# Four-layer vision network: layers 3 and 0 of neighbouring images run as one row of chunks, two scan states per instruction

## Chip, cores and metric

The kernel runs on one core of a Trainium2 chip. The metric is the device time of one execution in microseconds (us); smaller is better. Engine names follow the profile: PE is TensorE (matmuls; PEld are its weight loads), DVE is VectorE, ACT is ScalarE, POOL is GpSimd, SP is the queue that issues DMAs.

## What is computed

Four images of 64 channels and 64 x 64 pixels go through four layers, all in float32:

```python
x = layer0(x)   # cross-shaped conv, relu, layernorm, mamba with 16 states, + residual
x = layer1(x)   # two mambas with 96 states, along rows and along columns, + residual
x = layer2(x)   # content-dependent 3x3 high-pass filter, + residual
x = layer3(x)   # mamba with 16 states, projection, layernorm, silu, + residual

# the mamba of layers 0 and 3, per image (L = 4096 tokens, d_inner = 128, 16 states):
xz = h @ in_proj.T; xm, z = split(xz)
xc = silu(causal_conv4(xm) + b)
dt, B, C = split(xc @ x_proj.T)            # 4, 16 and 16 columns
dt = softplus(dt @ dt_proj.T + b)
for t in range(L):                         # A = -exp(A_log)
    h = h * exp(dt[t] * A) + (dt[t] * xc[t]) * B[t]
    y[t] = h @ C[t]
y = (y + xc * D) * silu(z)
```

The state of layer 0 begins at zero for each image. That of layer 3 runs on from image to image, because its reference flattens the batch into one sequence; so do the three tokens that its convolution looks back to.

## The kernel before

Images are done one after the other: `image(b)` calls `layer0`, `layer1`, `layer2`, `layer3`. Layers 0 and 3 hold the tokens of an image in 8 chunks of 512 (`TOK`), channels on partitions. They share two functions.

`mamba_front` makes, for one chunk, what the scan needs: the convolution (4 matmuls into `pc`), the gate (`pz`), both silus in one tile of 128 x 1024 (`sl`), the step size (`pd`, then a softplus as a polynomial of degree 6 on DVE) and `wx`, the product of step size and input.

`mamba_scan` goes through the 16 states of the chunk one by one. For each state PE makes two broadcasts over the partitions, B into `pb` and C into `pq`, each a 128 x 128 by 128 x 512 matmul with a weight tile `xb` whose columns are all the same. ACT makes the decay `a` (an exponential), DVE makes `g` = `pb` times `wx`, the scan `h` along the tokens, and `o` = `pq` times `h`. POOL saves the last column of `h` as the state and adds `o` to `y`. Broadcast tiles rotate over four PSUM banks, `a`, `g`, `h` and `o` over three buffers each.

`layer0` wraps this with the cross-shaped convolution (5 matmuls, `px`), relu (`seq`), the layernorm (`pm`, `pv`, `rsqrt_eps`) in front, and behind it the output projection `po`, the residual into `x1`, and a transposed copy on POOL. `layer3` adds the projection `po`, a layernorm, a silu, the residual on POOL and the DMA to the output behind each chunk. In both, the front of chunk c + 1 is traced before the scan of chunk c, and the tile framework's scheduler orders the instructions of an engine from there. Layer 1 alone fixes its order: `in_order` ties each instruction of PE, DVE, ACT and POOL to the one traced before it on that engine.

A matmul in float32 leaves two records in the trace, one for each of two passes over its columns.

Of the kernel before, what the change touches and what calls it, by code (L numbers as in the profile page):

```python
# [20 lines left out]
HW = H * W  # L21
# [33 lines left out]
LOG1P = (  # L55
    0.9999987483024597,
    -0.4998696446418762,
    0.3310944736003876,
    -0.23503851890563965,
    0.1492237150669098,  # L60
    -0.0664016604423523,
    0.014140978455543518,
)


class Net:
    def __init__(self, ctx, tc, a):
        self.tc, self.nc, self.a = tc, tc.nc, a
        nc = self.nc
        self.const = ctx.enter_context(tc.tile_pool(name="const", bufs=1))  # L70
        self.xp = ctx.enter_context(tc.tile_pool(name="xp", bufs=1))
        with tc.tile_pool(name="setup", bufs=1) as sp, tc.tile_pool(
            name="setup_ps", bufs=2, space=PSUM
        ) as pp:
            self.setup(sp, pp)
        for b in range(NB):
            self.image(b)
# [25 lines left out]

    def silu(self, out, v, t):

        nc = self.nc
        nc.scalar.activation(t, v, AF.Abs)
        nc.scalar.activation(t, t, AF.Exp, scale=-1.0)
        nc.scalar.activation(t, t, AF.Ln, bias=1.0)
        nc.vector.scalar_tensor_tensor(t, v, 0.0, t, ALU.min, ALU.subtract)  # L110
        nc.scalar.activation(t, t, AF.Exp)
        nc.vector.tensor_tensor(out, v, t, ALU.mult)  # L112

    def softplus_steps(self, out, v, u, p):

        nc = self.nc

        def first():
            nc.scalar.activation(u, v, AF.Abs)
            nc.scalar.activation(u, u, AF.Exp, scale=-1.0)  # L120

        def second():
            nc.vector.tensor_scalar(p, u, LOG1P[6], LOG1P[5], ALU.mult, ALU.add)
            nc.vector.tensor_tensor(p, p, u, ALU.mult)
            for c in LOG1P[4:1:-1]:
                nc.vector.scalar_tensor_tensor(p, p, c, u, ALU.add, ALU.mult)

        def third():
            for c in LOG1P[1::-1]:
                nc.vector.scalar_tensor_tensor(p, p, c, u, ALU.add, ALU.mult)  # L130
            nc.vector.scalar_tensor_tensor(out, v, 0.0, p, ALU.max, ALU.add)

        return [first, second, third]
# [98 lines left out]
    def setup_mamba(self, sp, pp, n):  # L232
# [23 lines left out]
        m["xbc"] = self.load(self.const, f"{n}_xbc", [DIN, 2 * NST])  # L256
# [115 lines left out]
    def image(self, b):  # L372
        self.use_exp()
        x1 = self.layer0(b)
        x2 = self.layer1(b, x1)
        self.use_exp()
        x3 = self.layer2(b, x2)
        self.layer3(b, x3)


    def mamba_pools(self, ctx, n):
        tc = self.tc
        p = {}
        p["w"] = ctx.enter_context(tc.tile_pool(name=f"{n}_w", bufs=1))
        p["s"] = ctx.enter_context(tc.tile_pool(name=f"{n}_s", bufs=2))
        p["n"] = ctx.enter_context(tc.tile_pool(name=f"{n}_n", bufs=3))
        p["bc"] = ctx.enter_context(tc.tile_pool(name=f"{n}_bc", bufs=4, space=PSUM))
        p["ps"] = ctx.enter_context(tc.tile_pool(name=f"{n}_ps", bufs=4, space=PSUM))
        return p

    def mamba_bcast(self, p, m, n):

        t = p["w"].tile([DIN, 2 * NST, DIN], F32, name=f"{n}_xb", tag="xb")
        self.nc.vector.tensor_copy(t, m["xbc"].unsqueeze(2).to_broadcast([DIN, 2 * NST, DIN]))
        return t

    def mamba_front(self, p, m, src, n):

        nc = self.nc
        vec = m["vec"]  # L400
        pc = p["ps"].tile([DIN, TOK], F32, name=f"{n}_pc", tag="ps")
        for k in range(4):
            self.mm(pc, m["wk"][:, k, :], src(k), k == 0, k == 3)
        v = p["s"].tile([DIN, 2, TOK], F32, name=f"{n}_v", tag="v")
        nc.scalar.activation(v[:, 0, :], pc, AF.Identity, bias=vec[:, 4:5])
        pz = p["ps"].tile([DIN, TOK], F32, name=f"{n}_pz", tag="ps")
        self.mm(pz, m["wz"], src(3))
        nc.scalar.copy(v[:, 1, :], pz)
        t = p["s"].tile([DIN, 2, TOK], F32, name=f"{n}_t", tag="t")
        s = p["s"].tile([DIN, 2, TOK], F32, name=f"{n}_sl", tag="sl")  # L410
        self.silu(s, v, t)
        xc, sz = s[:, 0, :], s[:, 1, :]
        pd = p["ps"].tile([DIN, TOK], F32, name=f"{n}_pd", tag="ps")
        self.mm(pd, m["wdt"], xc)
        dv = p["s"].tile([DIN, TOK], F32, name=f"{n}_dv", tag="dv")
        nc.vector.tensor_scalar(dv, pd, vec[:, 5:6], None, ALU.add)
        u = p["s"].tile([DIN, TOK], F32, name=f"{n}_u", tag="u")
        q = p["s"].tile([DIN, TOK], F32, name=f"{n}_q", tag="q")
        dl = p["s"].tile([DIN, TOK], F32, name=f"{n}_dl", tag="dl")
        for step in self.softplus_steps(dl, dv, u, q):  # L420
            step()
        wx = p["s"].tile([DIN, TOK], F32, name=f"{n}_wx", tag="wx")
        nc.vector.tensor_tensor(wx, dl, xc, ALU.mult)
        return xc, dl, wx, sz

    def mamba_scan(self, p, m, xb, f, n):

        nc = self.nc
        xc, dl, wx, sz = f
        y = p["s"].tile([DIN, TOK], F32, name=f"{n}_y", tag="y")  # L430
        nc.gpsimd.tensor_scalar(y, xc, m["vec"][:, 6:7], None, ALU.mult)
        for i in range(NST):
            pb = p["bc"].tile([DIN, TOK], F32, name=f"{n}_pb{i}", tag="bc")
            self.mm(pb, xb[:, i, :], xc)
            pq = p["bc"].tile([DIN, TOK], F32, name=f"{n}_pq{i}", tag="bc")
            self.mm(pq, xb[:, NST + i, :], xc)
            a = p["n"].tile([DIN, TOK], F32, name=f"{n}_a{i}", tag="a")
            nc.scalar.activation(a, dl, AF.Exp, scale=m["A"][:, i : i + 1])  # L438
            g = p["n"].tile([DIN, TOK], F32, name=f"{n}_g{i}", tag="g")
            nc.vector.tensor_tensor(g, pb, wx, ALU.mult)  # L440
            h = p["n"].tile([DIN, TOK], F32, name=f"{n}_h{i}", tag="h")
            st = m["state"][:, i : i + 1]
            nc.vector.tensor_tensor_scan(h, a, g, st, ALU.mult, ALU.add)  # L443
            nc.gpsimd.tensor_copy(st, h[:, TOK - 1 : TOK])
            o = p["n"].tile([DIN, TOK], F32, name=f"{n}_o{i}", tag="o")
            nc.vector.tensor_tensor(o, pq, h, ALU.mult)  # L446
            nc.gpsimd.tensor_tensor(y, y, o, ALU.add)  # L447
        yz = p["s"].tile([DIN, TOK], F32, name=f"{n}_yz", tag="yz")
        nc.vector.tensor_tensor(yz, y, sz, ALU.mult)
        return yz  # L450

    def layer0(self, b):
# [3 lines left out]
        for r in range(0, H, 16):  # L456
            nc.sync.dma_start(xin[:, 1 + r : 17 + r, 1 : W + 1], self.a["x"][b, :, r : r + 16, :])

        x1 = self.xp.tile([2 * C, H + 3, W + 3], F32, name=f"x1_{b}", tag="xb")
        nc.gpsimd.memset(x1, 0.0)  # L460
        nc.vector.memset(self.m0["state"], 0.0)
        with ExitStack() as ctx:
            p = self.mamba_pools(ctx, f"a{b}")
            xb = self.mamba_bcast(p, self.m0, f"a{b}")
            hn = p["w"].tile([C, HW + 3], F32, name=f"hn{b}", tag="hn")
            nc.gpsimd.memset(hn[:, 0:3], 0.0)

            def front(c):
                n = f"a{b}_{c}"
                r0 = c * ROWS  # L470
                ps = p["ps"].tile([128, TOK], F32, name=f"{n}_px", tag="ps")
                for i, (dy, dx) in enumerate(((1, 1), (0, 1), (2, 1), (1, 0), (1, 2))):
                    self.mm(
                        ps[0:C], self.l0_wt[:, i, :],
                        xin[:, r0 + dy : r0 + dy + ROWS, dx : dx + W], i == 0, i == 4,
                    )
                seq = p["s"].tile([C, TOK], F32, name=f"{n}_seq", tag="seq")
                nc.scalar.activation(seq, ps[0:C], AF.Relu, bias=self.l0_b, scale=self.l0_s)
                pm = p["ps"].tile([128, TOK], F32, name=f"{n}_pm", tag="ps")
                self.mm(pm[0:C], self.cen64, seq)  # L480
                sq = p["s"].tile([C, TOK], F32, name=f"{n}_sq", tag="sq")
                nc.scalar.activation(sq, pm[0:C], AF.Square)
                pv = p["ps"].tile([128, TOK], F32, name=f"{n}_pv", tag="ps")
# [668 lines left out]
```

## Time and profile before

| | us |
|---|---|
| median of 3 runs | 20218.63 |
| lowest and highest run | 20208.28, 20228.49 |
| profiled execution, its own time | 20241.61 |
| span of its trace | 20239.9 |
| layer 0 of image 0 (36.6 to 567.1) | 530.5 |
| layers 3 and 0 between two layer 1 and 2 stages (4578.4 to 5608.7, 9616.8 to 10655.9, 14674.4 to 15703.9) | 1030.3, 1039.1, 1029.5 |
| layer 3 of image 3 (19719.7 to 20239.9) | 520.2 |

The boundaries are read from the first and last instructions of each layer in the timeline: a stretch of layers 3 and 0 begins with the first `d_pc` matmul and ends where layer 1 writes its first `A` tile. Busy time of an engine is the union of its records in a stretch. PEclk is the share of the full TensorE clock that was granted; a matmul's records get longer when it falls.

### The profile page before, as it was taken

Reading aid. Unit: us, or ns where it says so; the run is one execution under the profiler, and the core shown is the slowest. Engines: PE = TensorE matmul, PEld = TensorE weight load, DVE = VectorE, ACT = ScalarE, POOL = GpSimd, SP = SyncE. Lnnn points to the kernel's source line nnn. Section 1 sums busy time; section 2 is a strip of 40 time slices with the busy share of each in tenths; the row PEclk is TensorE's granted clock in tenths of the full one; section 3 lists DMA queues with packets and bytes.
Section 4 is the critical chain, followed back from the end, with each engine's and each line's share of the span. In section 5 each row is a group of like instructions: output and inputs, shape, how many; then the busy total and the mean of one; then the engine's idle time right before and its main releaser. Section 6 shows DMA issues by size and latency. Waiting matters only on the chain. (4 is left out here: it accounts for less than half of the span.)

```text
span 20239.9 us, 622630 instructions
## 1 busy us (share of the span) xinstructions
PE 18436.4 (91%) x269256; PEld 11821.8 (58%) x269256; DVE 16728.8 (83%) x20282; ACT 12294.7 (61%) x15342; POOL 10582.6 (52%) x8660
## 2 busy tenths in 40 slices
PE   7899999997799999999789999999977999999997
PEld 2666666662266666666226666666622666666652
DVE  7888878878888888887988888888798888788879
ACT  3577667763367766775336776777533677667753
POOL 4555545555555555555555554555555555455555
PEclk9999999998899999999889999999988999999998
DMA  0233333320023333332002333333200233333320
GB/s 6 64 82 82 81 77 81 81 70 4 1 67 83 83 77 80 81 82 66 4 1 70 83 82 75 81 81 82 65 4 1 72 83 82 75 81 81 83 63 2
DMA packets 558931, 1264.96 MB, mean 62 GB/s; under 512 B 159416, under 2 KB 160800, under 8 KB 556192
## 3 DMA queue, kind: packets, MB, share of 16 engines
q1 hardware_dynamic: 556192, 1225.12, 24.6%
q8 instruction: 2124, 34.80, 0.7%
q14 instruction: 615, 5.04, 0.1%
HBM read 6.24 MB, written 4.19 MB: 1 GB/s over the span
## 5 line engine op out<-in xcount | busy, mean ns | idle before, releaser
L857 ACT ACTIVATE b_k_e<-b_z,shift 128x768 f32<-128x768 f32 x6144 | 5532.2, 900 | 4474.7 <-PE b_z L158 3718.5
L865 POOL TENSOR_TENSOR b_k_tB<-b_BC,tri 128x512 f32<-128x512 f32 x3072 | 3437.7, 1119 | 7431.7 <-PE b_u_S L158 6664.8
L903 DVE TENSOR_TENSOR b_k_r<-b_u_S,b_k_r 128x768 f32<-128x768 f32 x6144 | 5860.2, 954 | 977.6 <-DMA b_k_r<-b_k_r 262.2
L880 DVE TENSOR_TENSOR b_k_e<-b_k_e,b_wt 128x768 f32<-128x768 f32 x6144 | 6176.4, 1005 | 29.2 <-ACT b_k_e L857 29.2
L158 PE MATMUL b_u_S<-b_k_e,b_k_tB 64*64 64x192 f32 x98304 | 5425.8, 335 | 583.8 <-DVE b_k_r L903 491.8
L857 ACT ACTIVATE b_k_r<-b_z,ln_eps 128x768 f32<-128x768 f32 x6144 | 5488.7, 893 | 0.0
L158 PE MATMUL b_y<-b_k_r,b_k_dC 64*64 64x192 f32 x98304 | 5192.2, 323 | 64.0 <-ACT b_yt L923 61.3
L158 PE MATMUL b_z<-A,b_T 48*64 48x384 f32 x49152 | 5215.4, 487 | 4.3 <-ACT b_k_r L857 4.1
L158 PEld LDWEIGHTS b_y<-b_k_r,b_k_dC 64*64 64x64 f32 x98304 | 3915.9, 133 | 2171.8 <-issue 1489.2
L865 POOL TENSOR_TENSOR b_k_dC<-b_BC,ident 128x512 f32<-128x512 f32 x3072 | 4755.9, 1548 | 3.3 <-DMA b_BC<-b_BC 1.9
L158 PEld LDWEIGHTS b_u_S<-b_k_e,b_k_tB 64*64 64x64 f32 x98304 | 3278.3, 132 | 1851.9 <-DVE b_k_r L903 1015.2
L158 PEld LDWEIGHTS b_z<-A,b_T 48*64 48x64 f32 x49152 | 1913.5, 134 | 225.5 <-DVE b_yg L772 57.8
L438 ACT ACTIVATE d_a<-d_dl,l_A 128x512 f32<-128x512 f32 x512 | 368.7, 721 | 1089.8 <-DVE d_h L443 1089.8
L438 ACT ACTIVATE a_a<-a_dl,l_A 128x512 f32<-128x512 f32 x512 | 367.9, 720 | 1052.1 <-DVE a_h L443 911.6
L447 POOL TENSOR_TENSOR a_y<-a_y,a_o 128x512 f32<-128x512 f32 x512 | 821.1, 1604 | 287.9 <-DVE a_o L446 274.0
L447 POOL TENSOR_TENSOR d_y<-d_y,d_o 128x512 f32<-128x512 f32 x512 | 758.8, 1482 | 221.8 <-DVE d_o L446 208.5
L158 PE MATMUL a_pq<-a_sl,a_xb 128*128 128x512 f32 x1024 | 626.2, 696 | 262.1 <-DVE a_o L446 151.7
L158 PE MATMUL d_pq<-d_sl,d_xb 128*128 128x512 f32 x1024 | 643.9, 715 | 232.3 <-DVE d_o L446 185.1
L158 PE MATMUL d_pb<-d_sl,d_xb 128*128 128x512 f32 x1024 | 650.3, 722 | 180.8 <-DVE d_o L446 177.6
L443 DVE TENSOR_TENSOR_SCAN d_h<-d_a,l_state,d_g 128x512 f32<-128x512 f32 x512 | 738.2, 1458 | 5.4
L443 DVE TENSOR_TENSOR_SCAN a_h<-a_a,l_state,a_g 128x512 f32<-128x512 f32 x512 | 697.9, 1365 | 17.2 <-ACT a_a L438 9.8
L158 PE MATMUL a_pb<-a_sl,a_xb 128*128 128x512 f32 x1024 | 605.9, 677 | 41.2 <-DVE a_o L446 38.1
(343 smaller groups left out, 12651.5 us busy)
## 6 DMA issues: line engine op xcount, KB each, us to landing
b_k_r<-b_k_r SPq DMA_DIRECT2D x6144, 192.0 KB, 3.0
b_BC<-b_BC SPq DMA_DIRECT2D x512, 12.0 KB, 1.9
xin<-in_x SPq DMA_DIRECT2D x16, 256.0 KB, 6.0
out<-d_so SPq DMA_DIRECT2D x32, 128.0 KB, 2.3
l1w_cw<-in_l1w_cw SPq DMA_DIRECT2D x1, 192.0 KB, 3.3
l1h_cw<-in_l1h_cw SPq DMA_DIRECT2D x1, 192.0 KB
t_l1w_in<-in_l1w_in SPq DMA_DIRECT2D x1, 144.0 KB, 2.2
t_l1w_xbc<-in_l1w_xbc SPq DMA_DIRECT2D x1, 144.0 KB
```

The lines of the kernel that those rows point to most:

```text
L158: self.nc.tensor.matmul(out, lhsT=lhsT, rhs=rhs, start=start, stop=stop)
L438: nc.scalar.activation(a, dl, AF.Exp, scale=m["A"][:, i : i + 1])
L443: nc.vector.tensor_tensor_scan(h, a, g, st, ALU.mult, ALU.add)
L447: nc.gpsimd.tensor_tensor(y, y, o, ALU.add)
L857: nc.scalar.activation(o.rearrange("p x (j c) -> p j x c", j=2), zin, AF.Sigmoid, bias=bias, scale=scale)
L865: nc.gpsimd.tensor_tensor(out, m.unsqueeze(3).to_broadcast(shape), x.unsqueeze(1).unsqueeze(2).to_broadcast(shape), ALU.mult,)
L880: nc.vector.tensor_tensor(e, e, chunks[q]["w"][:, i, :].unsqueeze(1).unsqueeze(2).to_broadcast([128, 2, 2, D1]), ALU.mult,)
L903: nc.vector.tensor_tensor(r, S[k][:, :, 0:UC], r, ALU.mult)
```

## The change

Layers 3 and 0 become generators of jobs. `layer3(b)` and `layer0(b + 1)` each return 8 chunks, every one with a list of `front` and (in `post`) way-out steps, and `mambas` runs the 8 chunks of layer 3 of an image and the 8 of layer 0 of the next image as one row. The first image's layer 0 and the last image's layer 3 run alone. The order on PE, DVE, ACT and POOL is the program order, through `in_order`.

The scan takes two states at a time, in 8 steps per chunk. `g` and `o` are one DVE instruction of 128 x 1024 for both states; the two scans and the two exponentials stay separate. B and C are no longer broadcast by matmuls of 128 rows with a weight tile of equal columns: one matmul per chunk (`pr`, with the weight `x4`) puts the rows of B and C at partitions 0, 32, 64 and 96 of a tile `bc`, and `spread` broadcasts one row with an 8-row matmul, whose weights are a column of the identity repeated 128 times. A call of `spread` is two such matmuls, at neighbouring 32-partition groups and into two PSUM banks. The sum over the states moves from POOL to PE: `y` is accumulated in PSUM by matmuls with the identity, one per state, opened by a matmul with diag(D). PSUM is used up: the two `spread` tiles (`bc0`, `bc1`) have two banks each and one buffer, and `y`, `ps`, `pl`, `pv` one bank each.

The front of the next chunk and the way out of the chunk before are dealt over 17 places, two in each step and one behind the last. Each front or post entry below is named with its place. Softplus now uses the rational form that layer 1 uses (Ln, Exp and two Squares on ACT, five DVE instructions), and some DVE instructions (`dv`, the affine steps of both layernorms) go to ACT. In layer 1 the softplus tile `ds` is gone, `s2` uses the place of `dl`. `x1` is zeroed at its borders only.

```diff
-        for b in range(NB):
-            self.image(b)
+        self.use_exp()
+        self.mambas("a", 0, None, None)
+        for b in range(NB):
+            x2 = self.layer1(b, self.x1)
+            self.use_exp()
+            self.mambas(f"d{b}", b + 1, b, self.layer2(b, x2))
...
+            self.spread(p, jobs[0], 0, 0)
+            for job, after in zip(jobs, jobs[1:] + [None]):
+                places = [[] for _ in range(17)]
+                for at, f in after["front"] if after else ():
+                    places[at].append(f)
+                for at, f in before["post"] if before else ():
+                    late = before["m"] is self.m3 and after is not None and after["m"] is self.m0
+                    places[at + 5 if late and at > 1 else at].append(f)
+                sums = self.scan(p, job, after, places, sums, last)
+                before = job
...
+    def spread(self, p, job, x, i):
+        ps = p["ps"].tile([DIN, 2, TOK], F32, name=f"{job['n']}_bc{x}{i}", tag=f"bc{x}")
+        for t in range(2):
+            r = 64 * x + 32 * t
+            pick = self.ident[r : r + 8, r + i : r + i + 1].to_broadcast([8, DIN])
+            self.mm(ps[:, t, :], pick, job["bc"][r : r + 8])
+        job["ps", x] = ps
...
+        a = decay(0)
+        for i in range(NST // 2):
+            self.spread(p, job, 1, i)
+            if i == 1:
+                job["y"] = p["ps"].tile([DIN, TOK], F32, name=f"{n}_y", tag="y")
+                self.mm(job["y"], m["D"], xc, True, False)
+            if sums:
+                sums()
+            g, h, o = T("g"), T("h"), T("o")
+            nc.vector.tensor_tensor(g, job["ps", 0], wide, ALU.mult)
+            now, a = a, decay(i + 1) if i + 1 < NST // 2 else None
+            for f in places[2 * i]:
+                f()
+            for t in range(2):
+                st = m["state"][:, 2 * i + t : 2 * i + t + 1]
+                nc.vector.tensor_tensor_scan(
+                    h[:, t, :], now[:, t, :], g[:, t, :], st, ALU.mult, ALU.add
+                )
+            nc.gpsimd.tensor_copy(m["state"][:, 2 * i : 2 * i + 2], h[:, :, TOK - 1])
+            if i + 1 < NST // 2:
+                self.spread(p, job, 0, i + 1)
+            elif after:
+                self.spread(p, after, 0, 0)
+            for f in places[2 * i + 1]:
+                f()
+            nc.vector.tensor_tensor(o, job["ps", 1], h, ALU.mult)
+            def sums(i=i, o=o):
+                for t in range(2):
+                    self.mm(
+                        job["y"], self.ident, o[:, t, :], False, i == NST // 2 - 1 and t == 1
+                    )
+            if i == NST // 2 - 1:
+                for f in places[16]:
+                    f()
+            self.in_order(last)
...
+        return list(
+            zip(at, (conv, conv_out, gate, silu1, silu2, silu3, soft1, rows, soft2, soft3))
+        )
...
+            job["front"] = [
+                (0, cross(0)), (1, cross(1)), (2, relu), (3, square), (4, root), (5, newton),
+                (5, scaled),
+            ] + self.mamba_front(
+                p, job, lambda k: hn[:, t0 + k : t0 + k + TOK], (6, 7, 8, 8, 10, 11, 12, 13, 14, 15)
+            )
...
+            job["post"] = [(1, out1), (2, out2), (4, out3)]
...
+            job["front"] = self.mamba_front(
+                p, job, lambda k: x3[:, t0 + k : t0 + k + TOK], (4, 5, 6, 6, 8, 9, 10, 11, 12, 13)
+            )
...
+            job["post"] = [
+                (1, out1), (2, out2), (3, square), (4, mean),
+                *self.norm(p, n, t, self.l3_pb, None, (5, 7)),
+                (7, silu1), (9, silu2), (11, silu3),
+            ]
...
-            s2 = T([128, NTL, D1], "ds", bufs=1)
-            d0 = dl[:, :, 0:D1]
+            d0 = s2 = dl[:, :, 0:D1]
```

The first pair of `front` and `post` is layer 0's, the second layer 3's. The numbers are places; `norm` returns `root` and `newton`. `cross(0)` and `cross(1)` are 3 and 2 matmuls of the cross-shaped convolution; `conv` is 4 matmuls, `gate`, `rows`, `relu`, `square` or `mean`, `out2` and `silu3` of the front one each; `newton` is 3 DVE instructions, `soft3` 5, `soft2`, `silu2`, `silu3`, `out1`, `out3` one each.

## The prediction

> **What bounds the kernel now.** I read the page's first two parts, the timeline for the boundaries of the layers, the busy time by stretch for each layer, and the groups by shape.
>
> ```profile
> span 20239.9 us, 622630 instructions
> PE 18436.4 (91%) x269256; PEld 11821.8 (58%) x269256; DVE 16728.8 (83%) x20282; ACT 12294.7 (61%) x15342; POOL 10582.6 (52%) x8660
> PEclk9999999998899999999889999999988999999998
> ```
>
> The second row averages unlike stages. The stretches separate them (us; then busy time of PE, PEld, DVE, ACT, POOL; then the granted clock):
>
> ```profile
> 569.00:4457.00 3888.00, 3704.30 (x65514) 2650.66 (x65517) 3237.26 (x3903) 2711.26 (x3328) 2023.92 (x1570) 0.99 0.33 80
> 4665.60:5079.90 414.30, 306.74 (x540) 102.66 (x539) 392.40 (x457) 149.64 (x213) 238.67 (x237) 0.87 0.01 3
> 5208.80:5605.90 397.10, 317.29 (x609) 105.46 (x608) 363.82 (x447) 135.39 (x187) 241.14 (x238) 0.92 0.00 0
> sum 4149.60, PE 3155.59 PEld 1043.84 DVE 3593.27 ACT 1404.19 POOL 2249.85; mean PE 631.12 PEld 208.77 DVE 718.65 ACT 280.84 POOL 449.97
> ```
>
> Layer 1 takes 3888 us per image and is not what changes. Rows two and three are seven chunks of layer 3 and of layer 0: 59.2 and 56.7 us each, with DVE busy 95% and 92%. The last row sums all five stretches of layers 3 and 0: 4149.6 us, a fifth of the span, is all that the change can work on. DVE is slowed there by POOL:
>
> ```profile
> L447 POOL TENSOR_TENSOR d_y<-d_y,d_o 128x512 f32<-128x512 f32 x512 | 758.8, 1482 | 221.8 <-DVE d_o L446 208.5
> L443 DVE TENSOR_TENSOR_SCAN d_h<-d_a,l_state,d_g 128x512 f32<-128x512 f32 x512 | 738.2, 1458 | 5.4
> L440 DVE TENSOR_TENSOR d_g<-d_pb,d_wx 128x512 f32<-128x512 f32 x512 | 343.0, 675 | 26.3 <-PE d_pb L158 24.1
> ```
>
> The scan's mean is 1458 ns, its median 1275, its longest 2309: the long ones lie beside POOL's `y` additions. PE has spare time, but see its clock:
>
> ```profile
> 301.35 1.13 PE L158 MATMUL a_pq<-a_sl,a_xb 128*128 128x512 f32 x2
> 302.32 1.02 PE L158 MATMUL a_pb<-a_sl,a_xb 128*128 128x512 f32 x2
> 4487.76 8.98 PE L158 MATMUL c_p<-x,l_w 64*32 64x512 f32 x36
> ```
>
> At full clock a matmul of 512 columns (two records) follows the last after 0.86 us. Layer 2's two halves (rows 0 to 63 and 64 to 127) run at the same time: 18 matmuls in 8.98 us.
>
> ```profile
> 4500.20:4510.40 10.20, 10.20 (x14) 3.81 (x12) 5.17 (x12) 0.26 (x1) 7.58 (x7) 0.50 0.00 0
> 4578.70:4585.50 6.80, 6.80 (x9) 2.65 (x10) 4.36 (x1) 0.00 (x0) 6.68 (x4) 0.50 0.00 0
> 4513.80:4517.30 3.50, 3.50 (x12) 0.72 (x10) 0.00 (x0) 0.00 (x0) 2.52 (x2) 0.51 0.00 0
> 4517.30:4527.50 10.20, 10.20 (x43) 3.85 (x40) 3.08 (x7) 0.68 (x1) 2.24 (x2) 1.00 0.00 0
> ```
>
> PE is busy without a gap in all four. With 18-row matmuls (`c_pk`, row one) and 64-row ones (`d_pc`, row two) the clock stays at half; with two 64-row halves at once (row three) it is full one stretch later (row four). I weighted the streaming time in every 3.41 us stretch of the trace by rows/128: from half clock the next stretch was full where that share was 0.82 or more (11 exceptions in 563), from full clock it was half below 0.42 (20 in 5333). Rows decide, not busy time.
>
> **The change, part by part.** DVE durations, free of POOL: a 512-element instruction 0.60 us behind an independent one and 0.72 behind the one that it needs (`d_q`: three in 2.15), 1024 elements 1.13 and 1.24 (`d_t`, 1.20 at best), a scan 1.19 and 1.30. A step of two states is g 1.24, scans 2.49, o 1.13: 4.86 us, against 2 x 2.39 = 4.78 before. Merging wins nothing on DVE; the gain is POOL's absence, and fewer softplus instructions. Front and way out add 10.6 (layer 3) and 10.0 (layer 0): DVE needs 49.5 and 48.9 us of the 59.2 and 56.7.
>
> PE gets more. Per step: `spread` of C, two `sums`, `spread` of the next B, where before four full matmuls stood. `sums` are 1.71. No row shows 128-column matmuls in two row groups at once. As `c_p`'s halves a pair takes 0.86, one after the other 1.71; I take 0.86, its tiles too lying in different rows and banks, and keep 1.71 for a rival. Between tile shapes the trace has gaps from 0.09 (`a_pz` to `a_pq`) to 0.2 (`b_y` to `b_z` at 2001.3); I take 0.18, twice a step. PE needs 3.8 us a step, plus 10 or 16 matmuls of 0.86 a chunk: 40 and 46 us.
>
> PE and DVE nearly tie, so order decides. In program order C's `spread` waits for the last `o` (one buffer), and the next B's `spread` stands behind it, the sums and the even place; it is ready 4.0 us (0.86 + 0.18, 1.71 + 0.18, 0.86, 0.2 until its end is seen) plus that place's matmuls after the last `o`, and the next `g` waits for it. Walked at full clock, a step is the longer of 4.86 plus its DVE extras and 4.0 plus its PE extras, plus any lag carried in:
>
> - Layer 3: 5.5, 5.8 (diag(D), `out2`), 8.3 (`conv` and `mean`, 4.5), 6.8 (`newton`), 9.1 (`silu2` and `silu3`, with 1.2 waiting for their Exp, which ACT has queued behind layer 3's second silu), 5.5, 8.8 (`soft2`, `soft3`), 4.9: 54.7 us.
> - Layer 0: 6.8 (`cross`), 8.5 (`cross(1)`, diag(D), `relu`, `out2`), 7.5 (`newton`, `out3`), 7.6 (`conv`), 4.9, 8.6 (silu), 4.9, 8.7 (softplus): 57.5 us.
>
> Heads and tails of the five rows, from the same rows of before (a first front 30 us for layer 3, 48 for layer 0, ends of 6 to 17): 217 us. Sum at full clock: 32 x 54.7 + 32 x 57.5 + 217 = 3807, or 342 us less than 4149.6.
>
> Then the clock. A chunk's row-weighted work is 16 sums and 4 more full matmuls, 6 or 12 of 64 rows, and the 8-row `spread`s, which weigh 0.06 a row group or 0.25 if whole groups count: 21 to 27 of 54.7 us and 24 to 29 of 57.5, a share of 0.39 to 0.51. Before it was 0.54 and 0.60 (34 full and 6 or 12 half matmuls in 59.2 and 56.7 us), with whole-stage clocks of 0.84 and 0.85. Stretches below 0.42 are certain where DVE holds PE: steps 4 and 6 of layer 3 (PE idle 4.4 and 5.0 us), steps 2, 5 and 7 of layer 0 (3.7 to 4.1). Full clock returns only in 2.8 us of 128-row matmuls within one stretch. At half clock the two sums last 3.43 us, which a free-running stretch catches in about 4 of 10 steps; step 1, with diag(D) and sums in a row, catches it nearly always. Priced per step at half against full (a plain step 7.3 for 4.9, `conv` 14 to 16 for 8, `cross` 12.7 for 6.8) and by these odds: 7 us a chunk in layer 3 (steps 5, 7, 0, 1), 13 in layer 0 (0, 1, 3, 4, 6). 32 x 20 = 640 us.
>
> Here a rule and the rows part. The Trainium skill, "TensorE: Matmul & The Clock Gate", Part 1, lets any busy stretch of about 3.4 us restore full clock. By it each of the five idles costs one half stretch, 1.7 us: 272 us in all, and the change gains 70. By the rows above, spreads and 64-row matmuls restore nothing: it loses 298. I take the rows. "TensorEngine Tiling (Array Packing)", Key Properties, says that a change of tiling mode drains the array; my 0.18 is this trace's price of that.
>
> Costed at nothing: `xin`'s zeroing (3.7 us of POOL) and its four DMAs move ahead of layer 3 on POOL and SP, 400 us before use, and nothing else there waits for them; uncovered, about 10 us a row. ACT has some 30 us of work a chunk; only the Exp above is late. Layer 1's `s2` in `dl` adds no instruction; `dl` was last read a chunk earlier. One activation table load (1.28 us) an image goes.
>
> Sum: 20239.9 - 342 + 640 = 20538. The profiled run's own time, 20241.6, lies 23 above the median: 20218.6 + 298, about 20520.
>
> **Rivals.**
> 1. The clock holds, the likeliest way to be faster. Place: steps 4 and 6 of layer 3, 2, 5 and 7 of layer 0. Price: at zero loss 19880, with before's clock (2 to 3.5 us a chunk) about 20050. It decides where the loss is under 342/64 = 5.3 us a chunk. For it: 128-row sums stand in every step. Against: the share falls below before's.
> 2. Half clock becomes the regular state: then PE bounds every step, 78 and 88 us a chunk, up to 21600; half way there, 21000. For it: the slower a chunk, the smaller its share, so the state feeds itself. Against: step 1 restores it once a chunk.
> 3. The pairs of `spread` run one after the other: 1.71 us more a step, some 6 us a chunk after DVE's slack, about 20990 with the clock's loss.
>
> **How the numbers follow.** Forecast 0.47 (loss of 7 to 16 us a chunk, 20320 to 20900), rival 1 0.24, rivals 2 and 3 0.12 each, no change 0.05. A change is told from none here beyond 0.2%, 40 us. Faster 0.24, same 0.05, slower 0.71. From 19900, rival 1's better end, to 21250, inside rival 2, less than 2 in 10 is left out. Both signs hold weight, so the forecast's own range stands above.
>
> **What would show it.** POOL in these stretches falls from 2250 us to a few hundred, scans go to 1.27 us, DVE idles on PE's `bc` tiles. Clock in layers 3 and 0: 0.6 to 0.75 if I am right, over 0.84 for rival 1, under 0.6 for rival 2. Starts of the two `spread` matmuls of a pair: together, or 0.86 apart for rival 3. I am wrong if the clock holds and the stretches still take over 1030 us, or if layer 1 moves.

## The result, and the profile after

| | before | after |
|---|---|---|
| median, us | 20223.56 (4 runs, 20208.28 to 20244.11) | 20508.99 (4 runs, 20484.25 to 20573.57) |
| profiled execution, its own time | 20241.61 | 20573.57 |
| five stretches of layers 3 and 0 | 4149.6 | 4496.8 |
| the rest of the span | 16090.3 | 16075.1 |

The changed kernel takes 1.0145 times as long, 95% interval 1.0119 to 1.0172. The forecast was 20520 and slower; the loss lies where it was put, in the stretches of layers 3 and 0 (+347 us). The rest of the span is 15 us shorter.

The page of the changed kernel, its span, its first busy row and its row of granted clocks:

```profile
span 20571.9 us, 623348 instructions
PE 19353.3 (94%) x271560; PEld 11962.9 (58%) x271560; DVE 16230.0 (79%) x18936; ACT 12513.5 (61%) x15787; POOL 8659.2 (42%) x7064
PEclk7899999996689999999769999999966999999996
```

DVE and POOL have less work than before (16230 us for 16729, 8659 for 10583), PE has more, and the clock falls to six and seven tenths wherever layers 3 and 0 stand. The busy time by stretch, in the columns used before: layer 1 of the first image, seven chunks of layer 3, seven of layer 0, and then the sum over all five stretches of layers 3 and 0:

```profile
643.00:4530.00 3887.00, 3708.33 (x65650) 2654.73 (x65650) 3235.45 (x3909) 2713.97 (x3331) 2021.60 (x1568) 0.99 0.32 81
4731.00:5189.90 458.90, 426.75 (x827) 126.64 (x828) 342.66 (x328) 188.06 (x281) 26.84 (x64) 0.67 0.01 2
5275.40:5753.30 477.90, 445.33 (x860) 129.15 (x860) 325.09 (x303) 154.14 (x226) 46.02 (x65) 0.70 0.00 0
sum 4496.80, PE 4093.73 PEld 1197.52 DVE 3095.07 ACT 1623.64 POOL 330.31; mean PE 818.75 PEld 239.50 DVE 619.01 ACT 324.73 POOL 66.06
```

Layer 1 has not moved (3887 us for 3888). A chunk of layer 3 takes 65.6 us (458.90 / 7) for 59.2, one of layer 0 68.3 for 56.7, at clocks of 0.67 and 0.70 for 0.87 and 0.92. These windows run from the first chunk's `yz` to the eighth's. In the changed kernel layer 3's window so holds the seam, where the last chunk of layer 3 carries the first front of layer 0, and layer 0's holds the last chunk, which carries no front. From the first `g` of a chunk to that of the next one of the same layer (28 chunks of each) it is 62.5 us for 60.2 in layer 3 and 73.2 for 61.3 in layer 0. By this count the 347 us are 332 in layer 0's chunks and 64 in layer 3's, 41 at the heads and ends of the rows, and a gain of 90 at the three seams: from the last layer 3 chunk's first `g` to layer 0's it took 109 us before, and 80.5, 80.4 and 75.5 after. Running the two layers as one row has paid; the steps have lost more.

POOL went from 2250 us to 330 and DVE from 3593 to 3095, as meant. PE went from 3156 to 4094 and is busy in 93% of both windows. The groups of instructions say who waits for whom:

```profile
L417 DVE TENSOR_TENSOR_SCAN d_h<-d_a,l_state,d_g 128x512 f32<-128x512 f32 x512 | 629.1, 1270 | 24.9 <-DVE d_g L411 2.0
L411 DVE TENSOR_TENSOR a_g<-a_bc,a_wx 128x1024 f32<-128x1024 f32 x256 | 312.2, 1219 | 596.9 <-PE a_bc L120 596.3
L411 DVE TENSOR_TENSOR d_g<-d_bc,d_wx 128x1024 f32<-128x1024 f32 x256 | 312.2, 1219 | 406.5 <-PE d_bc L120 403.7
```

The scan is at 1270 ns throughout, where its mean was 1458: POOL no longer slows it. But DVE now stands idle for 1000 us (596.3 + 403.7) in front of `g`, until PE has written B's `spread`. Before, the two rows of `g` had 129 us of that (24.1 in layer 3, and 105.3 in layer 0):

```profile
L440 DVE TENSOR_TENSOR a_g<-a_pb,a_wx 128x512 f32<-128x512 f32 x512 | 341.5, 672 | 108.2 <-PE a_pb L158 105.3
```

The timeline of PE in one chunk of layer 3 (start, length, then the matmuls; the changed kernel):

```profile
4860.67 4.15 PE L120 MATMUL d_bc<-d_bc,ident 8*128 8x512 f32 x8
...
4870.99 1.14 PE L120 MATMUL d_bc<-d_bc,ident 8*128 8x512 f32 x8
4872.06 1.98 PE L120 MATMUL d_y<-d_o,ident 128*128 128x512 f32 x4
...
4886.85 2.07 PE L120 MATMUL d_bc<-d_bc,ident 8*128 8x512 f32 x4 [3.08 <-DVE d_o L427]
4888.86 3.78 PE L120 MATMUL d_y<-d_o,ident 128*128 128x512 f32 x4
4892.57 2.08 PE L120 MATMUL d_bc<-d_bc,ident 8*128 8x512 f32 x4
4894.57 2.08 PE L120 MATMUL d_pd<-d_sl,l_wdt 128*128 128x512 f32 x2
4896.58 2.08 PE L120 MATMUL d_bc<-d_bc,ident 8*128 8x512 f32 x4
4898.59 3.78 PE L120 MATMUL d_y<-d_o,ident 128*128 128x512 f32 x4
```

At full clock two sums (four records) last 1.98 us, and from 4870.99 even the `spread`s of B and of C for one step, four matmuls, lie in 1.14 us. At 4883.8 PE waits 3.08 us for `o`, and the clock is lost. From there two sums last 3.78 us and a pair about 2.08, and although PE runs on without a gap, the clock stays at half for the next 40 us:

```profile
4886.90:4927.60 40.70, 40.70 (x64) 11.38 (x64) 31.74 (x31) 16.39 (x26) 3.53 (x6) 0.50 0.02 3
```

That is the state that the prediction priced.

### The profile page after: what moved, and what is told of

It is laid out like the page before. It is cut to its first block, busy times and chain, and to the rows that moved or that the text cites. A ratio compares the mean times of both kernels' runs of the same rounds, so it can differ in the third digit from the quotient of the medians.

```text
span 20571.9 us, 623348 instructions
## 1 busy us (share of the span) xinstructions
PE 19353.3 (94%) x271560; PEld 11962.9 (58%) x271560; DVE 16230.0 (79%) x18936; ACT 12513.5 (61%) x15787; POOL 8659.2 (42%) x7064
## 5 line engine op out<-in xcount | busy, mean ns | idle before, releaser
L420 POOL COPY l_state<-d_h 128x2 f32<-128x2 f32 x256 | 72.2, 282 | 2018.1 <-DVE d_h L417 2018.1
L120 PE MATMUL a_bc<-a_bc,ident 8*128 8x512 f32 x2048 | 728.9, 847 | 154.9 <-DVE a_o L427 150.0
L120 PE MATMUL d_bc<-d_bc,ident 8*128 8x512 f32 x2048 | 721.7, 913 | 148.2 <-DVE d_o L427 121.6
L420 POOL COPY l_state<-a_h 128x2 f32<-128x2 f32 x256 | 92.1, 360 | 1753.4 <-DVE a_h L417 1751.7
L120 PE MATMUL d_y<-d_o,ident 128*128 128x512 f32 x1024 | 821.3, 948 | 1.9 <-DVE d_o L427 1.9
L120 PE MATMUL a_y<-a_o,ident 128*128 128x512 f32 x1024 | 811.1, 939 | 2.5 <-DVE l_state L547 1.9
L411 DVE TENSOR_TENSOR a_g<-a_bc,a_wx 128x1024 f32<-128x1024 f32 x256 | 312.2, 1219 | 596.9 <-PE a_bc L120 596.3
L417 DVE TENSOR_TENSOR_SCAN d_h<-d_a,l_state,d_g 128x512 f32<-128x512 f32 x512 | 629.1, 1270 | 24.9 <-DVE d_g L411 2.0
L417 DVE TENSOR_TENSOR_SCAN a_h<-a_a,l_state,a_g 128x512 f32<-128x512 f32 x512 | 628.8, 1269 | 20.9
L411 DVE TENSOR_TENSOR d_g<-d_bc,d_wx 128x1024 f32<-128x1024 f32 x256 | 312.2, 1219 | 406.5 <-PE d_bc L120 403.7
```

What stands on the lines that cost most here:

```text
L120: self.nc.tensor.matmul(out, lhsT=lhsT, rhs=rhs, start=start, stop=stop)
L411: nc.vector.tensor_tensor(g, job["ps", 0], wide, ALU.mult)
L417: nc.vector.tensor_tensor_scan(h[:, t, :], now[:, t, :], g[:, t, :], st, ALU.mult, ALU.add)
L420: nc.gpsimd.tensor_copy(m["state"][:, 2 * i : 2 * i + 2], h[:, :, TOK - 1])
```

## The experiments

Chunk times in the text below are those of windows of seven chunks, divided by 7; the clock is that of the window. The last column has the time from `g` to `g`, without seams and last chunks. Every ratio is to the kernel before, run on the same chip. The chips differ: the kernel before took 20209 to 20225 us on them, so a difference between medians of two chips is uncertain by some 16 us.

| kernel | median us | ratio, 95% | layer 3: chunk, clock | layer 0: chunk, clock | `g` to `g`: layer 3, layer 0 |
|---|---|---|---|---|---|
| before | 20224 | 1 | 59.2, 0.87 | 56.7, 0.92 | 60.2, 61.3 |
| after | 20508.99 | 1.0145 (1.0119 to 1.0172) | 65.6, 0.67 | 68.3, 0.70 | 62.5, 73.2 |
| e1_rows32 | 20237.73 | 1.0013 (1.0007 to 1.0020) | 60.7, 0.80 | 63.6, 0.82 | 57.4, 66.5 |
| e2_rows128 | 20258.28 | 1.0023 (1.0013 to 1.0032) | 62.9, 0.95 | 61.9, 0.99 | 60.6, 65.5 |
| e3_order8 | 20247.89 | 1.0013 (1.0006 to 1.0020) | 65.2, 0.72 | 58.9, 0.81 | 61.9, 63.7 |
| e4_quad32 | 19914.70 | 0.9854 (0.9839 to 0.9868) | 55.7, 0.87 | 57.1, 0.88 | 54.5, 60.0 |
| f2_quad8 | 20299.77 | 1.0037 (1.0024 to 1.0050) | 61.5, 0.71 | 62.8, 0.76 | 57.4, 67.4 |
| f1_fill | 20366.93 | 1.0070 (1.0055 to 1.0085) | 62.9, 0.83 | 64.4, 0.86 | 60.9, 67.8 |
| g3_fill8 | 21082.86 | 1.0430 (1.0413 to 1.0447) | 73.0, 0.68 | 77.9, 0.67 | 71.8, 81.3 |
| b1_ysum | 20281.74 | 1.0032 (1.0023 to 1.0042) | 58.4, 1.00 | 61.2, 1.00 | 58.7, 62.7 |
| f3_places | 19969.03 | 0.9876 (0.9862 to 0.9891) | 55.4, 0.87 | 58.9, 0.84 | 53.0, 62.5 |
| g1_next32 | 20123.37 | 0.9953 (0.9939 to 0.9968) | 60.4, 0.80 | 59.7, 0.82 | 57.3, 62.9 |
| g2_mixed32 | 19989.64 | 0.9886 (0.9871 to 0.9901) | 55.6, 0.86 | 59.1, 0.83 | 53.1, 62.9 |
| h1_quadfill | 19826.57 | 0.9802 (0.9786 to 0.9819) | 55.7, 0.91 | 54.4, 0.94 | 53.9, 56.6 |

**Is it the clock? More rows of zeros (e1, e2).** `bc` holds 8 rows of values from each of partitions 0, 32, 64 and 96, and zeros between them. e1 lets every `spread` read 32 rows, 24 of them zero, which add nothing: the same instructions in the same order.

```diff
-            pick = self.ident[r : r + 8, r + i : r + i + 1].to_broadcast([8, DIN])
-            self.mm(ps[:, t, :], pick, job["bc"][r : r + 8])
+            pick = self.ident[r : r + 32, r + i : r + i + 1].to_broadcast([32, DIN])
+            self.mm(ps[:, t, :], pick, job["bc"][r : r + 32])
```

> Only the spread changes: each of its matmuls reads 32 rows instead of 8 (the 24 added rows are zero on both sides, so the values, the time of a matmul, every wait and the order stay as they are). Theory, the granted clock follows streaming time weighted by rows: a pair then weighs 0.5 instead of 0.125, the clock in layers 3 and 0 rises from 0.67 to 0.80-0.85, chunks fall from about 63 and 70 us to 58-60 and 62-64, and the time from 20509 to about 20120 (20000 to 20250). Rival, the clock follows PE's busy time, or the order alone sets the time: same clock, 20509 within 40.

e2 reads all 128 rows (`self.ident[:, r + i : r + i + 1]` broadcast, and the whole of `bc`), so that two matmuls of a pair no longer lie in different rows and run one after the other.

> Each spread matmul reads all 128 rows, so the two of a pair can no longer run at the same time: PE gets 1.7 us more work in each of the 8 steps of a chunk, everything else stays. Theory, the clock is what the change lost: clock 0.95 or more, 60 and 66 us a chunk from the step sums at full clock, about 20265 (20150 to 20400), so faster than the changed kernel although PE does about a quarter more. Rival, PE's amount of work and its order are what was lost: 6 to 12 us more a chunk, 20900 to 21300.

The seven chunks of layer 3 and of layer 0, for e1, then for e2:

```profile
4705.00:5129.80 424.80, 353.38 (x823) 109.24 (x824) 340.49 (x328) 188.25 (x281) 30.41 (x64) 0.80 0.01 3
5198.70:5644.00 445.30, 384.28 (x860) 116.62 (x860) 324.38 (x303) 154.73 (x226) 46.00 (x65) 0.82 0.00 0
```

```profile
4694.90:5135.10 440.20, 393.46 (x828) 153.23 (x827) 341.67 (x328) 187.81 (x281) 24.31 (x64) 0.95 0.01 2
5202.90:5636.20 433.30, 395.83 (x860) 150.29 (x859) 325.13 (x303) 155.07 (x227) 46.01 (x65) 0.99 0.00 0
```

With the rows alone, e1 is 271 us faster than the changed kernel (20508.99 - 20237.73), and the clock rises from 0.67 and 0.70 to 0.80 and 0.82. PE's busy time in the two windows falls from 872 us to 738 with the same instructions. The time lies inside the range, but 118 us above the 20120 expected: not all steps get their clock back. e2 gives PE 0.85 us more work in each of two pairs a step and is still 251 us faster than the changed kernel; from `g` to `g` its chunks take 60.6 and 65.5 us, where 60 and 66 had been expected. So at least some 270 us of the change's time is clock.

**What does order cost? (e3, e4, f2).** In the changed kernel the next B's `spread` stands behind C's, diag(D), both sums and the even place. e3 moves it ahead of the sums:

```diff
             self.spread(p, job, 1, i)
+            g, h, o = T("g"), T("h"), T("o")
+            nc.vector.tensor_tensor(g, job["ps", 0], wide, ALU.mult)
+            if i + 1 < NST // 2:
+                self.spread(p, job, 0, i + 1)
+            elif after:
+                self.spread(p, after, 0, 0)
             if i == 1:
...
-            if i + 1 < NST // 2:
-                self.spread(p, job, 0, i + 1)
-            elif after:
-                self.spread(p, after, 0, 0)
             for f in places[2 * i + 1]:
```

> Order alone: the spread of the next B is put in front of diag(D), the sums and the step's place, still with 8 rows. If the late B spread is the cause, DVE's waits for it go, chunks come to 50-52 us at the clock of the changed kernel or better, about 19850. If the clock is the cause, PE's work of 40 and 46 us a chunk at a clock of 0.65 to 0.7 still takes 60 to 68 us: 20300 to 20500, with the clock not above 0.7.

```profile
4669.20:5125.30 456.10, 374.17 (x827) 118.31 (x828) 341.09 (x327) 186.17 (x279) 22.26 (x63) 0.72 0.01 2
5204.90:5617.00 412.10, 341.97 (x856) 108.36 (x856) 323.19 (x303) 154.12 (x226) 43.74 (x65) 0.81 0.00 0
```

It came out between the two expectations: 261 us faster than the changed kernel (20508.99 - 20247.89), nearly all of it in layer 0 (58.9 us for 68.3). That its clock would stay low was wrong for layer 0, at 0.81. The same rows in a shorter chunk are a larger share of it, which would account for that; order and clock are then not independent.

e4 takes another order and 32 rows at once: the sums first, then `g`, then C's and the next B's `spread` together, four matmuls side by side.

```diff
-            self.spread(p, job, 1, i)
             if i == 1:
...
             if sums:
                 sums()
             g, h, o = T("g"), T("h"), T("o")
             nc.vector.tensor_tensor(g, job["ps", 0], wide, ALU.mult)
+            self.spread(p, job, 1, i)
+            if i + 1 < NST // 2:
+                self.spread(p, job, 0, i + 1)
+            elif after:
+                self.spread(p, after, 0, 0)
...
-            if i + 1 < NST // 2:
-                self.spread(p, job, 0, i + 1)
-            elif after:
-                self.spread(p, after, 0, 0)
             for f in places[2 * i + 1]:
```

> Both together, and the two spreads of a step side by side behind the sums, so that their four matmuls of 32 rows lie in four row groups and can run at once (weight 1, 0.86 us for four). Theory: PE needs 33 and 38 us a chunk, its weighted share is 0.52 to 0.57, clock 0.8 to 0.9, DVE bounds the chunk at 51 to 54 us: about 19600 (19450 to 19850), faster than both kernels. Rival, a four-way spread does not overlap or DVE waits for the later C spread: over 20000.

f2 is e4 with the 8 rows of the changed kernel:

> The order of e4_quad32 with the changed kernel's own spreads of 8 rows: the fourth corner of (old order, sums first) x (8 rows, 32 rows). Theory (rows set the clock, and the clock sets the time in either order): the clock of the seven chunks falls from 0.87 and 0.88 to 0.65 to 0.75 in layer 3 and layer 0, the chunks take 60 to 63 us, and the kernel 20100 to 20250. Rival (with this order the chunks are bound by DVE and the Exp waits, so that the clock no longer costs): 19915 as e4_quad32, with a clock near 0.7 and the chunks at 55.7 and 57.1 us.

Seven chunks of layer 3 and of layer 0, of e4, then of f2:

```profile
4652.60:5042.80 390.20, 274.70 (x826) 87.25 (x826) 339.41 (x327) 187.57 (x280) 24.32 (x64) 0.87 0.01 3
5106.70:5506.10 399.40, 300.71 (x864) 94.85 (x860) 322.33 (x304) 156.09 (x228) 46.16 (x66) 0.88 0.00 0
```

```profile
4699.20:5129.40 430.20, 338.48 (x834) 104.21 (x834) 341.55 (x326) 187.39 (x280) 24.22 (x64) 0.71 0.01 2
5210.20:5650.00 439.80, 342.73 (x864) 106.00 (x860) 322.53 (x304) 156.11 (x228) 46.23 (x66) 0.76 0.00 0
```

e4 beats both kernels, though by less than expected; the ratio of 0.9854 is a gain of about 300 us on before. Between f2 and e4 only the rows differ, and with them 5.7 and 5.8 us a chunk, 0.16 and 0.12 of clock, and 385 us in all (20299.77 - 19914.70). The chunks of f2 were as expected; its total is 50 us above the range's end. The rival, that in this order the clock no longer costs, falls. The groups of e4 show where the wait of 1000 us went:

```profile
L427 DVE TENSOR_TENSOR a_o<-a_bc,a_h 128x1024 f32<-128x1024 f32 x256 | 312.4, 1220 | 257.0 <-PE a_bc L120 253.3 <-issue 0.6 <-DVE a_h L421 0.5
L427 DVE TENSOR_TENSOR d_o<-d_bc,d_h 128x1024 f32<-128x1024 f32 x256 | 311.6, 1217 | 92.5 <-PE d_bc L120 85.7
L410 DVE TENSOR_TENSOR a_g<-a_bc,a_wx 128x1024 f32<-128x1024 f32 x256 | 310.5, 1213 | 0.1
```

`g` waits for next to nothing (0.1 us in layer 0, 0.4 in layer 3), and `o` waits 339 us (253.3 + 85.7) for C instead.

**The clock from the idle side (f1, g3).** f1 keeps the order and the 8 rows and fills PE's idle time: four matmuls of a zero weight tile, 128 rows, into `y`.

```diff
+        self.zero = self.ctile([DIN, DIN], "zero")
+        nc.vector.memset(self.zero, 0.0)
...
+            if after and i in ((2, 5, 7) if after["m"] is self.m0 else (4, 6)):
+                for _ in range(4):
+                    self.mm(job["y"], self.zero, xc, False, False)
```

> The changed kernel, its order and its 8-row spreads as they are, with four more 128-row matmuls of zero weights, accumulated into y, in two steps of a layer 3 chunk and three of a layer 0 chunk (7 and 10 us of PE at full speed; they add zero and change nothing else). Theory (a loss of the clock, from too few rows streaming): the clock of the seven chunks rises from 0.67 and 0.70 to 0.85 or more, and the kernel comes to 19950 to 20250 in spite of more work for PE. Rival (PE's work in its order is the bound, the clock only goes along): 20509 plus up to 128 chunks of 7 to 10 us = 20509 to 21500.

g3 changes one thing in it, `self.mm(job["y"], self.zero[:8], xc[:8], False, False)`:

> f1_fill with one change: the same added matmuls read 8 rows of the zero weights instead of 128. They are as many, in the same places, and keep PE busy as long. Theory (the clock follows rows, not busy time): the clock of the seven chunks stays at 0.70 or below, 8-row matmuls in the idle steps bring nothing, and the kernel takes 20500 to 21000. Rival (any work in the idle steps holds the clock): 0.83 and 0.86 and 20367 as f1_fill.

f1, then g3 (layer 3, layer 0), and from g3's timeline one fill of four matmuls:

```profile
4711.50:5151.80 440.30, 412.66 (x948) 133.69 (x949) 342.42 (x327) 186.89 (x280) 27.14 (x63) 0.83 0.01 2
5225.60:5676.70 451.10, 434.46 (x1004) 139.00 (x1004) 323.84 (x304) 156.08 (x228) 46.17 (x66) 0.86 0.00 0
```

```profile
4826.70:5337.40 510.70, 483.30 (x944) 153.93 (x945) 343.48 (x328) 188.50 (x281) 22.40 (x64) 0.68 0.01 2
5415.20:5960.20 545.00, 534.24 (x1004) 168.45 (x1004) 325.36 (x303) 154.46 (x226) 45.99 (x65) 0.67 0.00 0
```

```profile
5460.80 7.03 PE L120 MATMUL a_y<-a_sl,zero 8*128 8x512 f32 x8
```

f1 adds 596 matmuls, 513 us of PE at 0.86 us each, and the kernel is 142 us faster than the changed kernel (20508.99 - 20366.93). The clock came to 0.83 and 0.86; the time stayed 117 us above the range. The fill stands in PE's queue ahead of the next C's `spread`, and `o`'s wait for C went from 54 us in the changed kernel to 150, while `g`'s wait for B fell from 1000 to 724. With 8 rows the same fill holds PE for 7.03 us at half clock, the clock does not move (0.68, 0.67), and the kernel is 716 us slower than f1 and 83 above the range expected for it. PE's busy time is no help; the rows are.

**POOL's relief alone (b1).** The kernel before, with `y` summed on PE:

```diff
-        p["ps"] = ctx.enter_context(tc.tile_pool(name=f"{n}_ps", bufs=4, space=PSUM))
+        p["ps"] = ctx.enter_context(tc.tile_pool(name=f"{n}_ps", bufs=3, space=PSUM))
+        p["y"] = ctx.enter_context(tc.tile_pool(name=f"{n}_y", bufs=1, space=PSUM))
...
-        y = p["s"].tile([DIN, TOK], F32, name=f"{n}_y", tag="y")
-        nc.gpsimd.tensor_scalar(y, xc, m["vec"][:, 6:7], None, ALU.mult)
+        y = p["y"].tile([DIN, TOK], F32, name=f"{n}_y", tag="y")
+        self.mm(y, m["D"], xc, True, False)
...
-            nc.gpsimd.tensor_tensor(y, y, o, ALU.add)
+            self.mm(y, self.ident, o, False, i == NST - 1)
```

> The kernel before, with one thing changed: y is summed by PE in PSUM (a matmul with diag(D), then one with the identity for each state) and no longer by POOL; one PSUM buffer of the front's goes to y. This is the change's relief of POOL alone, with the one-state steps and the old spreads. Theory (POOL beside DVE is what stretched the scans, and 128-row matmuls keep the clock): scans near 1.27 us throughout, POOL in the stretches of layers 3 and 0 from 2250 us to under 500, clock above 0.95 there, chunks of 53 to 56 us, and 19950 to 20150. Rival (PE, with 16 more matmuls of 0.86 us a chunk, about 50 us of work, becomes what DVE waits for): 20224 or more, DVE's idle time before g and o behind PE.

The two windows, and two groups of the whole trace:

```profile
4676.00:5084.60 408.60, 364.66 (x783) 135.41 (x781) 361.55 (x457) 149.96 (x213) 45.70 (x119) 1.00 0.01 3
5205.00:5633.40 428.40, 396.11 (x853) 143.74 (x851) 347.03 (x447) 138.34 (x187) 57.92 (x120) 1.00 0.00 0
```

```profile
L446 DVE TENSOR_TENSOR_SCAN d_h<-d_a,l_state,d_g 128x512 f32<-128x512 f32 x512 | 651.4, 1277 | 38.5 <-DVE d_g L443 0.5
L449 DVE TENSOR_TENSOR a_o<-a_pq,a_h 128x512 f32<-128x512 f32 x512 | 348.1, 685 | 289.6 <-PE a_pq L158 274.5
```

The scan comes to 1277 ns and the clock to 1.00, as the theory said, and still the kernel is slower than before, as the rival said. The `y` sums stand in PE's queue among the broadcasts, and `o` of layer 0 waits 274.5 us for C behind them (51.0 before). One buffer of the front's went with the change; how much of the wait is that buffer's was not separated. Relieving POOL is worth something on DVE (31 and 17 us of busy time in seven chunks), and layer 3 is a little shorter for it (58.4 us for 59.2); what waits for PE in layer 0 takes more than that back, even with no clock lost.

**Where is the best order? (f3, g1, g2, h1).** f3 deals e4's front later:

```diff
-(6, 7, 8, 8, 10, 11, 12, 13, 14, 15)
+(6, 7, 8, 8, 10, 12, 13, 13, 15, 16)
...
-(4, 5, 6, 6, 8, 9, 10, 11, 12, 13)
+(4, 5, 6, 6, 8, 10, 11, 11, 13, 14)
```

> e4_quad32 with the front's places dealt later: in layer 3 (4,5,6,6,8,10,11,11,13,14) for (4,5,6,6,8,9,10,11,12,13), in layer 0 (6,7,8,8,10,12,13,13,15,16) for (6,7,8,8,10,11,12,13,14,15), so that DVE meets the second silu instruction after its Exp. Theory (that Exp is what layer 3's steps 3 and 4 and layer 0's step 5 wait for, 3 to 5 us a chunk): 19750 to 19880, steps 3 and 4 of layer 3 together from 18.5 to about 15 us, nothing else longer. Rival (the front's end is then too late for the next chunk's bc and decay): the first steps of a chunk lengthen by as much, and it is 19915 or more.

A miss: 19969, slower than e4. From `g` to `g`, layer 3's step 4 fell from 10.4 to 7.9 us and step 6 from 8.7 to 5.7, but steps 0, 5 and 7 grew by 1.1, 1.4 and 1.7. (Steps are means over the second to seventh chunk of every row.) In layer 0 step 1 grew from 8.3 to 12.3: there `o` waits for C, up to 8.2 us at a time and 63.6 us in the seven chunks, against 51.7 in e4.

g1 is e3 with 32 rows (the two lines of e1's diff):

> The order of e3_order8 (C's spread, then the next B's, both ahead of the sums) with spreads of 32 rows. Theory (rows are worth 270 to 385 us in every order): 19860 to 19980, clock 0.85 to 0.9 in the seven chunks, layer 0 at 55 to 56 us a chunk, below e4_quad32's 57.1, layer 3 at 58 to 61. Rival (this order is bound by something else in layer 3, as its 65.2 us at 8 rows may show): layer 3 stays at 63 or more and the kernel above 20050.

A miss too: layer 0 stays at 59.7 us, and rows are worth only 125 us in this order (20247.89 - 20123.37). What DVE waits for in its seven layer 0 chunks (us in total, times, longest):

```profile
DVE a_t L473 <- ACT a_t L470: 27.0, 6, 4.5
DVE a_yz L609 <- PE a_y L120: 23.1, 8, 3.3
DVE a_o L427 <- PE a_bc L120: 22.5, 7, 5.2
DVE x L617 <- PE a_po L120: 17.7, 7, 3.3
```

With both spreads ahead of everything, the sums, the output projection and the silu's Exp on ACT (`a_t`) are late instead. With 8 rows, in e3, the same four waits are 27.0, 18.3, 18.6 and 17.4 us: in layer 0 they do not go when the rows come. g2 took that order in layer 0 alone, and e4's with f3's places in layer 3 (the two variants behind an `if m is self.m0`):

> An attempt at a version faster than e4_quad32 by layer: layer 0 in the order of e3_order8, layer 3 in the order of e4_quad32 with f3_places' places, all spreads of 32 rows. If the chunk times of the layers add up freely: layer 3 at 55.4 (f3_places), layer 0 at 55 to 56, 19800 to 19880. Rival (at the seams, and through the clock that one layer hands to the other, the gains are lost): 19915 or more.

It kept layer 3 at 55.6 us and brought layer 0 to 59.1, worse than e4's 57.1: 19990. Last, h1 is e4 with f1's fill, three matmuls (`range(3)`) placed ahead of the odd place:

> e4_quad32 with three more 128-row matmuls of zero weights into y in each of the steps where PE idles longest (steps 4 and 6 of a layer 3 chunk, steps 2, 5 and 7 of a layer 0 chunk): 5.2 and 7.7 us more work for PE a chunk. Theory (what is left of e4_quad32's distance from DVE's 49 us is partly its clock of 0.87 and 0.88): the clock comes to 0.95 or more, the chunks from 55.7 and 57.1 to 53.5 to 55 and 54.5 to 56, and the kernel to 19800 to 19870. Rival (that distance is waits for Exp and for PE's order, at any clock): the clock rises, the chunks stay within 0.5 us or grow, and it takes 19915 to 20000.

```profile
4622.10:5012.00 389.90, 316.07 (x916) 101.92 (x916) 340.63 (x327) 187.46 (x280) 24.32 (x64) 0.91 0.01 3
5074.10:5454.60 380.50, 330.18 (x962) 106.69 (x960) 321.54 (x304) 156.10 (x228) 46.19 (x66) 0.94 0.00 0
```

This is the fastest of all, 19826.57, a ratio of 0.9802 to before, with matmuls by zero added. The time is inside the range expected, the clock a little under the 0.95. The gain over e4 is in layer 0 (54.4 for 57.1 us a chunk). Layer 3 stayed at 55.7 at a higher clock, as the rival had it: its steps 4 and 6 take 10.4 and 8.7 us in both kernels, whatever the clock.

## Why the prediction was right, and where it was not

- **POOL's absence** came as told: 330 us of POOL, scans at 1270 ns, DVE down by 498 us (3593.27 - 3095.07).
- **PE's order sets the step.** The prediction had `g` wait for B's spread. The 1000 us in front of `g`, and their end in e4 (0.1 us for layer 0's `g`), show it. The walk of the steps at full clock cannot be read off the changed kernel itself; e2 is nearest to it, at 0.95 and 0.99, with pairs in series. The same steps with such pairs had been put at 60 and 66 us a chunk ahead of that run, and took 60.6 and 65.5 from `g` to `g`. The 0.18 us taken for a change of tile shape was 0.21 at full clock (4870.99 to 4872.06, of which 0.86 streams); in e2, where sums and spreads all have 128 rows, two sums are followed by the next matmul after 1.71 us, without such a gap.
- **The clock** was foreseen at 0.6 to 0.75 in layers 3 and 0; it was 0.67 and 0.70 in the windows and 0.63 to 0.74 over the five stretches. The rule read from the trace of before holds in the new one. From half clock, row-weighted shares with the bound at 0.82 name the next stretch with 24 exceptions in 1038; from full clock with the bound at 0.44, 23 in 4955. Busy time leaves 238 and 133. The bounds depend on how a matmul's streaming is laid out in time (by its columns alone, the upper one is 0.75); that rows tell more than busy time does not. Rows times columns would be a rival: counted like that, it does as well from half clock, but from full clock it leaves 63 exceptions for the rows' 16, and the `c_p` matmuls that the prediction shows, 64 rows by 32 columns and two at once, brought full clock with a share of 1 by rows and of 0.25 by rows times columns. This is where the Trainium skill, "TensorE: Matmul & The Clock Gate", Part 1, was set against the rows: by it the change gained 70 us, by the rows it lost 298. The loss measured is 285 us. The page and the traces differ, and the traces decide: 40 us without a gap at a clock of 0.50 in the changed kernel, and in g3 seven us of added work of 8 rows that restore nothing.
- **The weight of an 8-row spread** was left open between 0.06 and 0.25 a row group. Whole groups leave 84 and 65 exceptions against 24 and 23: the rows count, 0.06. e1 is what it would have been with 0.25.
- **The size of the clock's loss** was near in the sum, and partly by luck. From `g` to `g` layer 3 took 62.5 us a chunk for a forecast 54.7 + 7 = 61.7, layer 0 73.2 for 57.5 + 13 = 70.5: the loss was put 0.8 and 2.7 us a chunk too low, 97 us over 28 chunks of each. The heads, seams and last chunks, which the forecast took as chunks like the others and 217 us more, came to 47 us less than that. So the five stretches took 4496.8 us for 4447; and the profiled execution is the slowest of the four, 65 us above their median, which is more than this difference. The parts differ by step: from `g` to `g` layer 3 was slow in steps 1, 5, 6 and 7 (9.3, 8.0, 9.5 and 7.3 us against 5.8, 5.5, 8.8 and 4.9), and the prediction had 0 in place of 6; layer 0 in steps 0, 1, 3 and 6 (9.3, 13.8, 10.8 and 9.4 against 6.8, 8.5, 7.6 and 4.9) but not in step 4.
- **Pairs run together**, 1.14 us at full clock, so rival 3 falls. (Two sums of the prediction do not come out of their own terms, and neither enters the forecast: rival 3's 20990, where 64 chunks of 6 us on 20520 are about 20900, and PE's 40 and 46 us a chunk, which are 39 and 44.) Rival 2 does not come either, since step 1 with its diag(D) does restore the clock for a while: in step 2 of layer 3 it is 1.00 on the average. Rival 1, the clock held at 19880 to 20050, is near what e4 and h1 reach with another order and more rows.
- **What the walk did not tell about order.** It was made for one order, and the forecasts for others missed: e3 lies between the two theories, and rows were worth 271 us in the changed kernel's order, 385 in e4's and 125 in e3's, where 270 to 385 had been expected. Each order has its own next wait (C in e4; the silu's Exp, sums and projection in g1), and e3's shorter chunk also came with a fuller clock.

What stays open: even in h1 a chunk takes 53.9 and 56.6 us from `g` to `g`, 4.4 and 7.7 above the 49.5 and 48.9 that the prediction gave DVE. In layer 3 f3 took 5.5 us out of steps 4 and 6, and 4.2 came back in others; no kernel here removed both. Nor was it tried how h1's fill is best sized or placed.

## To carry to other kernels

When broadcasts or other small work is moved to TensorE matmuls of few rows, count the rows that stream and not only PE's busy time: a queue that never idles can sit at half clock. Where zeros are there to be read, read them: 32 rows in place of 8 cost nothing here and gave back 271 us. Before giving PE the sums of a step, see what is queued behind the wait for their input: with 8 rows, another order of sums and spreads was worth 261 us, some of it through the clock.

## What the runs showed of the hardware

- Rows of zeros count for the clock: with nothing but 24 of them added to every spread, the clock went from 0.67 and 0.70 to 0.80 and 0.82.
- Useless matmuls can make a kernel faster: three of 128 rows in two or three steps of a chunk, all by zero, took e4 from 19914.70 to 19826.57 us (0.9854 to 0.9802 of before). Four of 8 rows in the same steps of the changed kernel made it 574 us slower (21082.86 - 20508.99).
- Matmuls of 8 rows in four row groups (partitions 0, 32, 64 and 96), with different PSUM tiles, ran all four at once: 1.14 us at full clock for what takes 4 x 0.86 one after the other.
